# A three-layer recurrence and attention on one core: pipeline offsets of 8 and 16 turns, setup spread over turns, products in even units

## The chip, the cores and the metric

One core of a Trainium2 chip runs the whole program. The metric is the device time in microseconds (us) of one execution; it is given as the median of several runs. TensorE is PE in the profile (PEld is its weight loads), VectorE is DVE, ScalarE is ACT, GpSimd is POOL and SyncE is SP. SP issues most of the DMAs. Line numbers with an L are those of the kernel before.

## The reference, cut to what matters

A batch of 8 sequences of 512 tokens, 512 wide, goes through three recurrent layers and one attention layer. Each adds its output to its input. All numbers are float32.

```
x = x + L0(x)    # gated: needs h of the token before
x = x + L1(x)    # plain tanh recurrence
x = x + L2(x)    # plain tanh recurrence
x = x + L3(x)    # causal attention, 16 heads, one extra "image" key

L0 step: f = sigmoid([x_t, h] @ w_W + w_b); hid, o = split(f)
         m = x_t @ wx_W + wx_b + hid * (h @ wh_W + wh_b)
         h = o * h + (1 - o) * tanh(m)
L1, L2 step: h = tanh(x_t @ Wx + b + h @ Wh)
L3: q, k, v = split(x @ c_attn_w + c_attn_b)
    k_img, v_img = cond @ uk_w.T + uk_b, cond @ uv_w.T + uv_b
    scores = q @ [k_img, k].T / sqrt(32), causal, + mask
    out = softmax(scores) @ [v_img, v] @ c_proj_w + c_proj_b
```

## The kernel before

The program has two parts, one after the other. The first runs the recurrence; the second runs attention.

**Turns.** `turn(s)` (L660) does one token step of every layer that is live in turn s. Layer l works on token s - OFF[l]. With `OFF = (0, 2 * G + 1, 5 * G + 1)` and G = 4 (L22) the later layers are 9 and 21 turns behind layer 0. The loop (L743) runs s from -5 to 532, so after token 511 of layer 0 there are 21 more turns for the later layers. The order of the work on PE, DVE, ACT and POOL is the order in which it is written (a manual schedule); only SP's order is the scheduler's.

In a turn, PE runs in this order: `stream` twice (L547, tiles ph and po: h of layer 0 times its three gate matrices, each float32 product done as bfloat16 parts), `give0` (L490, tile pg0: a quarter of the input product of layer 0 for four coming tokens), `give12` (L503, tile pg1: the same for layers 1 and 2), `stream12` (L563, tile p12: h of the later layers), and `take` (L656, matmuls at L607). Every matmul uses 32 columns of the array; four of them, in the four column groups, run together.

DVE turns ph by 32 x 32 blocks (L572), sums the parts (L578), does the same with po, runs a scan (L688), forms `drop` (L703) and the new h (L704), and splits h into bfloat16 parts (`rest`, L463). ACT computes sigmoid and tanh between these. POOL forms `keep` (L702), which h also needs. When the new h is split, the next turn's ph can start. Then DVE turns and sums p12, ACT computes four tanh (L723), POOL splits the new h of the later layers (`rest` on POOL, L463) and adds it to x (L733): for layer 1 into xb, where layer 2 will read it, for layer 2 into xo.

**Input products.** `chunk_of` (L475) lets a layer's input product start `AHEAD` = G + 1 = 5 turns before the first of its four tokens, one quarter a turn. `given` (L514) turns a finished product into a tile `raw`, and `place` (L522) adds the bias and puts one token's share where the sums at L578 find it, one turn ahead. In a turn POOL does keep, place for layer 0 (two operations, L533), place for the later layers (L537), the x of layer 0 (L712), then the work of the later layers.

**Attention's q, k and v.** When layer 2 has finished a block of tokens (`BLOCKS`: seven of 64, then 32, 16, 16), `finish` (L617) stores x and queues `pieces`: for q and k eight products, for v some with 512 columns, each product made of KC = 4 pieces of four matmuls. `take(count)` runs pieces: one in three of four turns up to s = 511, three a turn after it. A finished product is copied from PSUM by ACT into one of two tiles e (L627, L645) and stored by SP (L631, L647). After the loop a flush (L753) runs what is left, eight pieces at a time.

**Setup.** `setup_loads` (after turn 513) starts the DMAs of attention's weights and masks, in room that layer 0's weights leave. `setup` (after turn 520) computes its constants in one go: the mask in three bfloat16 parts, some index tiles, the image keys (pk, L223), the image values (pi, L235), the output bias (pb, L245), and the mask sums.

**Attention.** `load(0)` (L792) loads q, k and v of batch 0 once the last block is stored. `run(g)` (L1009) works through 32 groups (8 batches of 4 groups with 4 heads each) in three slots: scores (L878, L884), maximum, exponential, transposes, and the products with v. `open_scores` (L841) computes the score of the image key for all four row blocks of a group.

Of the kernel before, what the change touches and what calls it, by code (L numbers as in the profile page):

```python
# [20 lines left out]
G = 4  # L21
OFF = (0, 2 * G + 1, 5 * G + 1)  # L22
AHEAD = G + 1
# [10 lines left out]
def cond_residual_kernel(  # L34
# [81 lines left out]
    def setup_loads():  # L116
# [38 lines left out]
        nc.gpsimd.memset(parts, 0.0)  # L155
# [5 lines left out]
    def setup(psum, tag):  # L161
# [7 lines left out]

        nc.vector.tensor_scalar(m0, m0, LOWEST, None, ALU.max)  # L170
# [10 lines left out]


# [29 lines left out]
        )  # L212

# [6 lines left out]
        for c in range(KC):  # L220
            pk = psum.tile([P, D], F32, tag=tag, name=f"pk_{c}")
# [11 lines left out]
        pi = psum.tile([P, D], F32, tag=tag, name="pi")  # L233
        for k in range(KC):
            nc.tensor.matmul(  # L235
                pi[0:B, :], ct[:, k, :], w_uku[:, 1, k, :], start=(k == 0), stop=(k == KC - 1)
            )
        nc.vector.tensor_tensor(vimg, pi[0:B, :], buv, ALU.add)
        nc.vector.tensor_tensor(vimg, vimg, bv, ALU.subtract)
        nc.vector.tensor_scalar(mt, mt, LOWEST, None, ALU.max)  # L240

        for c in range(KC):
            pb = psum.tile([P, D], F32, tag=tag, name=f"pb_{c}")
# [7 lines left out]
            )  # L251
        masks(0)
        for m in range(NQ - 1):
            beyond(0, m)
# [55 lines left out]
    with ExitStack() as rec:  # L310
# [164 lines left out]
        def chunk_of(l, s):  # L475

            at = s - OFF[l] + AHEAD
            return at - at % G, at % G
# [43 lines left out]
        def place(s, layers):  # L522
# [3 lines left out]
            share = raw[min(layers[0], 1), s - r - AHEAD + KC - 1][..., r * B : (r + 1) * B]  # L526
# [70 lines left out]
        def product(n, name, operands, width, done):  # L597


            ps = []  # L600
            for k in range(KC):
                def piece(k=k):
                    if not ps:
                        ps.append(psq.tile([P, D], F32, tag="q", name=f"pq_{name}"))
                    lhs, rhs = operands(k)
                    for j in range(KC):
                        nc.tensor.matmul(  # L607
                            ps[0][j * BP : (j + 1) * BP, 0:width],
                            lhs[:, j * BP : (j + 1) * BP], rhs,
                            start=(k == 0), stop=(k == KC - 1),  # L610
                        )
                    if k == KC - 1:
                        evict.append(lambda: done(ps[0][:, 0:width]))
                pieces.append(piece)

        def finish(n):
# [6 lines left out]
            for c in range(KC):  # L623
                for i in range(2):
                    def done(p, c=c, i=i):
                        e = ev.tile([P, D], F32, tag="e", name=f"e_{n}_{c}_{i}")
                        nc.scalar.activation(  # L627
                            e[:, 0 : B * size], p, AF.Identity,
                            bias=bcol[:, i, c : c + 1], scale=(qscale, 1.0)[i],
                        )  # L630
# [25 lines left out]
        def take(count):  # L656
            for _ in range(min(count, len(pieces))):
                pieces.pop(0)()

        def turn(s):  # L660
# [17 lines left out]
            take(int(s % 4 > 0) if s < T else 3)  # L678
# [29 lines left out]
            if [l for l in nxt if l]:  # L708
                place(s + 1, [l for l in nxt if l])
# [5 lines left out]
            if later:  # L715
# [12 lines left out]
                rest(nc.gpsimd, new12 if len(later) == 2 else new12[:, later[0] - 1])  # L728
# [6 lines left out]
            given(s, False)  # L735
            n = next((n for n in range(len(BLOCKS)) if s - OFF[2] + 1 == sum(BLOCKS[: n + 1])), None)
# [3 lines left out]
        with tc.manual_schedule(  # L740
            engines={nc.tensor.engine, nc.vector.engine, nc.scalar.engine, nc.gpsimd.engine}
        ):
            for s in range(-AHEAD, T + OFF[2]):  # L743
                n, at = divmod(s + AHEAD + 2 * G, TB)
                if at == 0 and 1 < n < NB:
                    load_x(n)
                turn(s)
                if s == TB:
                    load_qkv()
                if s == T + 1:  # L750
                    setup_loads()
                if s == T + 8:
                    setup(psq, "q")  # L753
            while pieces:
                take(2 * KC)
# [377 lines left out]
```

## Time and profile before

| | us |
|---|---|
| median of 3 runs (3559.51 to 3566.15) | 3562.95 |
| the profiled execution | 3555.52 |
| its span | 3553.4 |
| layer 0's last scan (L688) starts at | 2673.7 |
| last transposition of p12 (L572) starts at | 2796.2 |
| last matmuls of the flush (L607) end at | 2833.5 |
| first scores of attention (L878) start at | 2845.8 |
| PE busy / DVE busy / ACT busy / POOL busy | 3317.1 / 2436.9 / 1417.1 / 1283.2 |

The span lies between the first and the last instruction; the profiled execution's own time is 2.1 us longer. A turn of the recurrence can be read in the timeline from one start of ph to the next. Each line of the timeline has the start, the duration, the engine, the line, the operation with the tiles that it writes and reads, and in brackets the idle time before it and what ended that. In the table by windows, each line has the window, its length, and for every engine the busy time with the number of instructions, then the granted clock of PE, the DMA share and the rate.

### The profile page before, as it was taken

To read this page: it belongs to the slowest core of one execution; us is meant where nothing else is said; L and a number is where in the kernel's file an instruction comes from. 1 tells how busy PE (TensorE), PEld (TensorE's weight loads), DVE (VectorE), ACT (ScalarE), POOL (GpSimd) and SP (SyncE) were. 2 spreads that over 40 slices of the span, in tenths; PEclk is the share of its full clock that TensorE was granted. 3 is DMA by queue.
4 is the path that set the end of the run, shared out by engine and by line. 5 is a ranking of instruction groups with operands and counts; after the bars stand their busy time and mean duration, and the time that the engine had idled before them with its cause. 6 is when DMAs were issued, how large, how long until landed. Compare 5 with 4: busy or idle time off the path is not lost. (4 is left out here: it accounts for less than half of the span.)

```text
span 3553.4 us, 207431 instructions
## 1 busy us (share of the span) xinstructions
PE 3317.1 (93%) x91784; PEld 2417.4 (68%) x91784; DVE 2436.9 (69%) x7061; ACT 1417.1 (40%) x5179; POOL 1283.2 (36%) x4982
## 2 busy tenths in 40 slices
PE   4899999999999999999999999999998679999999
PEld 2677777777777777777777777777774445555555
DVE  4677777777777777777777777777773166777775
ACT  3233333333333333333333333333332156666664
POOL 2444444444444444444444444444442100100000
PEclk9999999999999999999999999999998979999999
DMA  4200010001001000100010001001012221222211
GB/s 126 54 8 7 8 24 18 16 16 34 16 17 28 16 20 17 28 16 19 16 28 16 22 20 25 16 17 28 13 31 50 51 102 53 63 68 73 63 37 25
DMA packets 197771, 116.30 MB, mean 33 GB/s; under 512 B 148684, under 2 KB 165092, under 8 KB 196860
## 3 DMA queue, kind: packets, MB, share of 16 engines
q1 hardware_dynamic: 191880, 100.92, 11.2%
q8 instruction: 721, 11.81, 1.4%
q10 hardware_dynamic: 4992, 2.11, 0.3%
q14 instruction: 178, 1.46, 0.1%
HBM read 61.02 MB, written 41.97 MB: 29 GB/s over the span
## 5 line engine op out<-in xcount | busy, mean ns | idle before, releaser
L547 PEld LDWEIGHTS <-h 128*32 128x32 bf16 x49152 | 1039.9, 97 | 371.8 <-DVE h L463 268.5
L723 ACT ACTIVATE h<-s 64x32 f32<-64x32 f32 x2048 | 535.8, 262 | 974.3 <-DVE s L578 946.7
L547 PE MATMUL ph<-v,h 128*32 128x256 bf16 x24576 | 771.9, 274 | 94.0 <-DVE h L463 79.1
L563 PE MATMUL p<-v,h 128*32 128x256 bf16 x24576 | 786.4, 273 | 20.9 <-POOL h L463 20.4
L463 POOL TENSOR_TENSOR h<-h 128x64 f32<-128x64 f32 (+1 forms) x1048 | 331.0, 316 | 1236.1 <-ACT h L723 1159.6
L563 PEld LDWEIGHTS <-h 128*32 128x32 bf16 x24576 | 674.2, 97 | 149.7 <-POOL h L463 34.3
L572 DVE STREAM_TRANSPOSE s<-ph 128x256 f32<-128x256 f32 x512 | 230.3, 450 | 374.3 <-PE ph L547 374.2
L490 PE MATMUL pg<-w0x,xb 128*32 128x384 f32 x4096 | 427.6, 491 | 24.5 <-DMA w0x<-in_wx_W_dram 10.6
L547 PE MATMUL po<-v0o,h 128*32 128x128 bf16 x24576 | 436.9, 220 | 0.0
L503 PE MATMUL pg<-w12x,xb 128*32 128x256 f32 x4096 | 321.4, 379 | 5.2 <-issue 3.5
L463 DVE TENSOR_TENSOR h<-h 128x32 f32<-128x32 f32 x1036 | 278.5, 270 | 35.9 <-DVE h L704 1.1
L572 DVE STREAM_TRANSPOSE s<-p 128x256 f32<-128x256 f32 (+1 forms) x524 | 232.6, 444 | 81.2 <-PE p L563 81.1
L578 DVE TENSOR_REDUCE sh<-s 128x64 f32<-128x320 f32 x512 | 249.0, 486 | 54.9 <-POOL h L463 2.8
L696 ACT ACTIVATE gates<-sh 128x32 f32<-128x32 f32 x512 | 119.6, 234 | 418.0 <-DVE sh L578 413.5
L607 PE MATMUL pq<-xo,w_qkv 128*32 128x512 f32 (+2 forms) x2560 | 273.4, 515 | 11.5 <-ACT e L627 11.5
L503 PEld LDWEIGHTS pg<-w12x,xb 128*32 128x32 f32 x4096 | 129.7, 110 | 210.6 <-issue 192.6
L578 DVE TENSOR_REDUCE s<-s 128x64 f32<-128x320 f32 (+1 forms) x524 | 254.7, 486 | 19.8
L702 POOL TENSOR_TENSOR keep<-og,h 128x32 f32<-128x32 f32 x512 | 139.8, 273 | 269.1 <-ACT og L699 269.0
L703 DVE SCALAR_TENSOR_TENSOR drop<-og,th 128x32 f32<-128x32 f32 x512 | 112.3, 219 | 155.2 <-ACT th L701 155.2
L878 PE MATMUL s<-qkt 32*128 32x384 f32 (+3 forms) x1024 | 155.3, 491 | 60.6 <-ACT prob L925 35.0
L911 DVE TENSOR_REDUCE rtop<-s 128x2 f32<-128x256 f32 (+3 forms) x256 | 205.0, 821 | 6.7
L975 ACT COPY pt<-tr 128x512 f32<-128x512 f32 x224 | 119.6, 588 | 187.1 <-PE tr L970 186.8
(155 smaller groups left out, 4206.6 us busy)
## 6 DMA issues: line engine op xcount, KB each, us to landing
qkt<-qk_out SPq DMA_DIRECT2D x16, 1024.0 KB, 5.7
qk_out<-e SPq DMA_DIRECT2D x56, 256.0 KB, 3.1
xin<-in_x_dram SPq DMA_DIRECT2D x128, 64.0 KB, 2.0
vt<-v_out SPq DMA_DIRECT2D x8, 1024.0 KB, 5.7
xr<-x_out SPq DMA_DIRECT2D x8, 1024.0 KB
out_dram<-res SPq DMA_DIRECT2D x128, 64.0 KB, 1.7
x_out<-xo SPq DMA_DIRECT2D x28, 256.0 KB, 5.3
v_out<-ev SPq DMA_DIRECT2D x56, 128.0 KB, 2.3
```

The source lines that it names most:

```text
L463: eng.tensor_tensor(part(h, i + 1), part(h, i), top(h, i), ALU.subtract)
L490: nc.tensor.matmul(pg[0][j * BP : (j + 1) * BP, :], tokens(t, c), w[:, j], start=(c == 0), stop=(c == KC - 1),)
L503: nc.tensor.matmul(pg[1][q * BP : (q + 1) * BP, :].rearrange("r (v n) -> r v n", v=2), tokens(t, c), w[:, u], start=(c == 0), stop=(c == K ...
L547: nc.tensor.matmul(out[j * BP : (j + 1) * BP, :], half(h, c), w[:, c, i].rearrange("p (g j n) -> p j g n", g=cols, j=KC)[:, j], start=(c = ...
L563: nc.tensor.matmul(out[q * BP : (q + 1) * BP, :].rearrange("r (v n) -> r v n", v=2), half(h[:, l - 1], c), w[:, u], start=(c == 0 and i == 0),
L572: nc.vector.transpose(to[:, :, :, 0 : NS - 1], p.rearrange("p (k b i) -> p k b i", b=B, i=NS - 1))
L578: nc.vector.tensor_reduce(to, parts, AX.X, ALU.add)
L607: nc.tensor.matmul(ps[0][j * BP : (j + 1) * BP, 0:width], lhs[:, j * BP : (j + 1) * BP], rhs, start=(k == 0), stop=(k == KC - 1),)
L702: nc.gpsimd.tensor_tensor(keep, og, part(old0, 0), ALU.mult)
L723: nc.scalar.activation(part(new12[v * 2 * BP : (v + 1) * 2 * BP, l - 1], 0), s_[fr, v * KC : (v + 1) * KC], AF.Tanh,)
L878: nc.tensor.matmul(pair[g, u, i // 2 * 2][:, i % 2, at : at + n], qkt[b][hs, 0, c, m * P : n], qkt[b][hs, 1, c, 0:n], start=True, stop=False,)
L911: nc.vector.tensor_reduce(top[:, k], s[:, :, at : at + (m + 1) * P], AX.X, ALU.max)
```

## The change

Six things are changed.

1. The offsets are `OFF = (0, 2 * G, 4 * G)`, that is 8 and 16, and the input products of the later layers start 4 turns ahead instead of 5 (`AHEAD = (5, 4, 4)`). The loop ends with turn 527. The input product of the later layers is now turned into `raw` in the same turn in which its first share is placed, so `place` for the later layers moves to the end of POOL's turn, behind `given`.
2. A piece is now a unit of at most 128 columns: a product 512 wide has 16 units instead of 4 pieces. `take` runs 3 units a turn while s < 496, 6 while s < 512, then 12. Units that follow each other in one k are run as one matmul (per column group).
3. `setup_loads` comes after turn 511. `setup` is a generator; from turn 512 on, turn 513 left out, two of its steps follow each turn. Its PSUM tiles are those of po and ph, which layer 0 no longer needs, and the image values are done in two halves.
4. From turn 512 on, the split of the later layers' h is done by DVE instead of POOL.
5. The flush uses matmuls with 128 columns of the array (`whole=True`), up to 16 units at a time; in the last block DVE instead of ACT copies the q products out of PSUM.
6. `load(0)` loads the first 384 tokens from POOL's queue and the last 128 from SP's. The image scores of group 0 are computed for row blocks 0 to 2 first and for block 3 ahead of the third slot. The pools of attention are created in another order, with waits by tile.

```diff
-OFF = (0, 2 * G + 1, 5 * G + 1)
-AHEAD = G + 1
+OFF = (0, 2 * G, 4 * G)
+AHEAD = (G + 1, G, G)
...
         def product(n, name, operands, width, done):
...
+            def stretch(k, at, end, whole=False):
+                if not ps:
+                    ps.append(psq.tile([P, D], F32, tag="q", name=f"pq_{name}"))
+                lhs, rhs = operands(k)
+                if whole:
+                    nc.tensor.matmul(
+                        ps[0][:, at:end], lhs, rhs[:, at:end],
+                        start=(k == 0 and at == 0), stop=(k == KC - 1), skip_group_check=True,
+                    )
+                for j in range(0 if whole else KC):
+                    nc.tensor.matmul(
+                        ps[0][j * BP : (j + 1) * BP, at:end],
+                        lhs[:, j * BP : (j + 1) * BP], rhs[:, at:end],
+                        start=(k == 0 and at == 0), stop=(k == KC - 1), skip_group_check=True,
+                    )
+                if k == KC - 1 and end == width:
+                    evict.append(lambda: done(ps[0][:, 0:width]))
...
-                pieces.append(piece)
+                for at in range(0, width, P):
+                    pieces.append((stretch, k, at))
...
-        def take(count):
-            for _ in range(min(count, len(pieces))):
-                pieces.pop(0)()
+        def take(count, whole=False):
+
+            units = [pieces.pop(0) for _ in range(min(count, len(pieces)))]
+            while units:
+                (stretch, k, at), n = units[0], 1
+                while n < len(units) and units[n] == (stretch, k, at + n * P):
+                    n += 1
+                stretch(k, at, at + n * P, whole)
+                units = units[n:]
...
-            take(int(s % 4 > 0) if s < T else 3)
+            take(3 if s < T - 4 * G else 6 if s < T else 12)
...
             if 0 in nxt:
                 place(s + 1, [0])
-            if [l for l in nxt if l]:
-                place(s + 1, [l for l in nxt if l])
...
-                rest(nc.gpsimd, new12 if len(later) == 2 else new12[:, later[0] - 1])
+                rest(nc.gpsimd if s < T else nc.vector, new12 if len(later) == 2 else new12[:, later[0] - 1])
...
             given(s, True)
             given(s, False)
+            if [l for l in nxt if l]:
+                place(s + 1, [l for l in nxt if l])
...
-                if s == T + 1:
+                if s == T - 1:
                     setup_loads()
-                if s == T + 8:
-                    setup(psq, "q")
+                    bits = setup(pst)
+                if s >= T and s != T + 1:
+                    for _ in range(2):
+                        next(bits, None)
+            for _ in bits:
+                pass
             while pieces:
-                take(2 * KC)
+                take(4 * KC, whole=True)
...
     def load(b):
...
+        cuts = (0, T - P, T) if b == 0 else (0, T)
+        for t0, t1 in zip(cuts, cuts[1:]):
+            eng = nc.sync if t1 == T else nc.gpsimd
+            for i in range(2):
+                eng.dma_start(
+                    qkt[b][:, i, :, t0:t1], qk_out[i, :, :, b, t0:t1].rearrange("c p t -> p c t")
+                )
+            eng.dma_start(
+                vt[b][:, t0 // P : t1 // P], v_out[b, t0:t1].rearrange("(m p) n -> p m n", p=P)
+            )
...
         for u, ks in enumerate(SLOTS):
             before = late[:]
             late.clear()
+            if g < 0 and u == 2:
+                open_scores(0, (3,))
...
         load(0)
-        open_scores(0)
+        open_scores(0, (0, 1, 2))
```

## The prediction

> **What bounds the kernel now.** I read the table by windows first, to see which stages there are.
>
> ```profile
> 1000.00:1500.00 500.00, 491.78 (x16120) 375.07 (x16116) 363.02 (x1118) 177.32 (x704) 225.66 (x875) 1.00 0.09 22
> 2800.00:2850.00 50.00, 25.50 (x448) 16.37 (x448) 2.95 (x10) 5.77 (x15) 0.00 (x0) 0.78 0.52 119
> ```
>
> In the recurrence PE (the first pair) is busy 491.8 of 500 us at full clock; around the flush it is busy half the time at clock 0.78. The timeline of PE shows a turn:
>
> ```profile
> 1501.15 1.03 PE L607 MATMUL pq<-xo,w_qkv 128*32 128x512 f32 x8
> 1502.01 1.48 PE L547 MATMUL ph<-v,h 128*32 128x256 bf16 x48
> 1503.99 0.82 PE L490 MATMUL pg<-w0x,xb 128*32 128x384 f32 x8
> 1505.06 1.48 PE L563 MATMUL p<-v,h 128*32 128x256 bf16 x48
> 1506.92 1.50 PE L547 MATMUL ph<-v,h 128*32 128x256 bf16 x48 [0.38 <-DVE h L463]
> 1508.91 0.82 PE L490 MATMUL pg<-w0x,xb 128*32 128x384 f32 x8
> 1511.30 1.03 PE L607 MATMUL pq<-xo,w_qkv 128*32 128x512 f32 x8
> ```
>
> From start to start: the turn at 1502.01 has no piece and lasts 4.91 us, and PE waits in it for h. Without that wait its work ends at p12 + 1.31 = 4.36. A piece adds 0.86 (1501.15 to 1502.01). Over turns 100 to 479 the timeline gives medians of 5.225 with a piece (285 turns) and 4.907 without (95). So three turns in four are bound by PE (4.367 + 0.858), and the fourth by the chain from ph over DVE and ACT to h. Layer 0's scans 80 and 496 are 2141.06 us apart: 5.147 a turn.
>
> POOL in the same stretch:
>
> ```profile
> 1503.66 0.71 POOL L463 TENSOR_TENSOR h<-h 128x64 f32<-128x64 f32 x2 [2.02 <-ACT h L723]
> 1504.32 0.27 POOL L733 TENSOR_TENSOR xb<-xb,h 128x32 f32<-128x32 f32 x1
> 1505.56 0.28 POOL L702 TENSOR_TENSOR keep<-og,h 128x32 f32<-128x32 f32 x1 [0.73 <-ACT og L699]
> 1506.25 0.31 POOL L537 TENSOR_TENSOR s<-raw,bias 128x64 f32<-128x64 f32 x1
> ```
>
> It is free for 0.73 us before keep. Then the tail, flush and start of attention:
>
> ```profile
> 2684.90 2.68 PE L563 MATMUL p<-v,h 128*32 128x256 bf16 x48 [2.17 <-POOL h L463]
> 2719.94 0.45 DVE L572 STREAM_TRANSPOSE s<-p 128x256 f32<-128x256 f32 x1 [3.50 <-PE p L563]
> 2735.16 5.81 PE L235 MATMUL pi<-room_b,ct 128*8 128x512 f32 x8
> 2749.55 0.45 DVE L572 STREAM_TRANSPOSE s<-p 64x256 f32<-64x256 f32 x1 [0.31 <-PE p L563]
> 2806.28 0.37 ACT L627 ACTIVATE e<-pq,bcol 128x128 f32<-128x128 f32 x1 [5.11 <-DMA qk_out<-e]
> 2820.47 0.37 ACT L627 ACTIVATE e<-pq,bcol 128x128 f32<-128x128 f32 x1 [5.64 <-DMA v_out<-ev]
> 2839.76 1.84 PE L846 MATMUL pim<-kb,qkt 128*128 128x4 f32 x8 [6.23 <-DMA v_out<-ev]
> 2845.83 1.24 PE L878 MATMUL s<-qkt 32*128 32x256 f32 x8 [4.23 <-DMA qkt<-qk_out]
> ```
>
> Two p12 transpositions lie at 2724.66 and 2749.55: 24.89 us for the one turn that holds the setup, against 4.72 for the turn before. The flush waits for stores that free the e tiles, and the first scores wait for the load of q and k.
>
> **Even units.** Three units are 384 of 512 columns: 0.75 x 0.858 = 0.644, and pg0, also 384 wide, measures 0.645 (1508.91 to the next start at 1509.56). A turn of PE is then 4.367 + 0.644 = 5.01. In two turns of four the three units span two k, so a matmul of 128 columns stands alone: 114 such records (14.25 groups of eight) of a product took 3.52 us, 0.247 a group against 0.215, so +0.03, and the mean gains 0.02. The chain must stay below: the new h is split 4.72 to 4.87 after ph starts (median 4.87), plus 0.05 to release PE, so 4.92 at most; it fits with 0.1 to spare.
>
> **The new wait.** With offset 16, layer 2 reads in turn s four tokens of which layer 1 wrote the last in turn s - 1; with 21 it had four more turns. This occurs once in four turns, at the second half of pg12. Layer 1's add into xb ends 7.98 after its turn's ph (median; 7.82 to 8.16). PE would start that half at 5.01 + 2.84 = 7.85. With 0.05 for the semaphore and 0.06 for the weights the wait is 0.1 to 0.4; I take 0.15, because place no longer stands among the operations that overlap the DVE split (the 4.72). p12, the units and the next ph are queued behind it on PE, so it counts in full: 0.04 a turn. Mean turn: 5.01 + 0.02 + 0.04 = 5.07; bounds 5.02 (no wait) and 5.13 (0.4 each time). 416 turns x (5.147 - 5.07) = **-32** (-53 to -7).
>
> The moved place ends POOL's turn: layer 2's add ends at 8.24, place takes 0.31 to 0.40, so 8.55 to 8.64; keep wants POOL at 5.07 + 3.555 = 8.63. It costs nothing as long as the 0.1 of the chain covers it.
>
> Turns 496 to 511 take six units: 4.367 + 1.5 x 0.858 = 5.65, against 75.71 / 15 = 5.05: **+9**. Layer 2 enters five turns earlier, at 0.2 more for each: **+1**.
>
> **Tail.** It runs from layer 0's last scan (2673.7) to the last p12 transposition (2796.2): 122.5 us. After, 16 turns. A turn with both layers and nothing in the way is 4.57 (2715.37 to 2719.94). But ACT copies products out before it does the tanh, and so waits until the units are through: 2701.70 to 2708.42 is 6.72 with a copy that waited for the third piece. The same sum with 12 units (2.58) and DVE's split (two operations of 0.3 instead of 0.69 on POOL) gives 5.5 where a product ends at 1.72 and 6.4 where it ends at 2.58. Turns 512 to 515: 5.5, 6.4, 5.5, 6.4. Turn 516 follows nine DVE operations of the mask and index steps (2.7 + 1.9 us by their rows): 7.0. Turn 517 has two pk, of which the second waits for DVE: 6.2. 518 and 519: 5.6, 6.5. Together 49. Layer 2 alone: 3.9 unhindered (2753.37 to 2757.26). Turn 520 has three copies of 0.37, the third waiting for an e tile (2.4 us to landing), and two pb: 7.4; 521: 6.3; 522 and 523: 5.3, 5.2; four at 3.8. Together 39. The setup's PE work (pk, pi, pb: 16 us, mostly at half clock) lies in the time in which PE waits for the tanh, except in turns 517 and 520, counted above; without that cover it would cost up to 16. setup_loads comes two turns earlier: SP issues 29 DMAs, the 16 of w_proj at 0.65 to 2 us, ahead of one or two stores of e. They are covered by the 14 us from one copy to the next; if not, one ACT copy and the tanh behind it lose up to 7.
>
> The clock: p12 took 2.68 instead of 1.49 after 2.17 us of idle PE (first line of the last fence); after 1.8 it ran at 1.16 for one layer, full speed. Turns 524 to 527 have no units, so PE idles 2.7 us in each, and I add 0.9 x 4 = 3.5. [...]
>
> 1.6 (rest of turn 511) + 49 + 39 + 3.5 = 93 to 95: **-28**. Bounds: 16 free turns (8 x 4.57 + 8 x 3.9 = 68) give -53; all 16 at 6.7 give -14.
>
> **Flush.** 2796.2 to 2833.5 is 37.3 us with 17 copies out of PSUM, 2.19 each, most of it the wait for an e tile's store. After, only the last block's 48 units are left, which are eight copies of q and k and one of v: 9 x 2.19 = 20: **-17**. Matmuls on the whole array change little: 117.6 us for 128 matmuls of 512 columns at L825 is 0.92, against 0.86 for four in parallel. Bounds: 9 copies at 3.5 (each waits its store in full) is -6; 1.2 each is -26.
>
> **Start of attention.** The first scores come 12.3 us after the flush's last matmul. The first 384 tokens can be loaded as soon as the last p12 has read the weights that lie in that room, some 20 us before the flush ends. No load on POOL's queue is in the trace; SP's of 1024 KB land after 5.7 us, and three of 768 KB should not need more than 17. Behind them on POOL stands nothing until `shares` of group 0. Then the first scores wait only for the last copy out of PSUM: 0.6, plus six image matmuls at half clock, 1.4: 2.5 after the flush. The last part lands some 9 us after it (v's eight stores issue until +6, +3 to land), and the third slot comes at +12. **-10** (0, if it is not covered, to -11).
>
> **Sum.** -32 + 9 + 1 - 28 - 17 - 10 = -77. Profiled execution: 3555.5 - 77 = 3478. It lies 7.4 below the median of the runs, and below all three, so I carry that over: 3563 - 77 = **3486**. The rest of attention is left as it is.
>
> **Rivals.** (A) The forecast, 3486, by itself 3465 to 3510: chance 0.68. (B) The evening gives nothing: layer 2's wait is 0.4 or more and the late keep lengthens the chain, so turns stay at 5.15: 3486 + 32 = 3518. For it: POOL's slack is below 0.1 by the rows; against it: a late keep first uses up the chain's own 0.1. 0.12. (C) Better: layer 2's wait is hidden (5.02, 21 less) and the tail runs near its free turns (20 less): 3445. For it: the 4.72 and 7.82 at the low end; against: the 6.72 turn. 0.13. (D) The early load is not early (it waits for the last stores, or POOL is slow to issue it): 3496. 0.04. (E) **Slower.** POOL becomes the loop: place now stands between layer 2's add and keep. From keep's start to the next ph are 1.36 us, so a turn of 5.28 needs keep at 3.92, 0.36 late in every turn, which means a place that ends at 9.2 instead of 8.6. From there on 416 x 0.13 eats the other 45 us and the whole is slower; with another 0.02 it is 3572. For it: a POOL split of 1.01 instead of 0.69 (2727.62, beside DVE's setup work); against: that is the only one, and it is half of what is needed. 0.03.
>
> **Range and chances.** About 0.2% (7 us) can be told from no change. (B) and half of (C) are to be held: 3446 to 3528. Faster: (A) to (D), less a little: 0.94; same 0.02; slower 0.04, with (E).
>
> **What would show it.** Right: turns of 5.05 to 5.1 of one length, with PE waiting once in four turns 0.1 to 0.2 us at the second half of pg12 for POOL; 16 tail turns in 94 us with no 25 us turn; nine copies in the flush; first scores 2 to 3 us after its last matmul. Wrong: turns of 5.15 or more with keep late; pk or pi waiting for a weight DMA; a copy waiting longer than 5 us in the tail; first scores still waiting for qkt.

## The result: a third of the gain that was forecast

The changed kernel takes 3535.29 us (median of four runs, 3534.39 to 3542.97) against 3562.97 for the kernel before on the same chip: a ratio of 0.9929, 95% interval 0.9917 to 0.9941, 27.7 us. The forecast was 77. In a later set of runs (`after_again`, below) it was 0.9959, 0.9943 to 0.9975.

One profiled execution of each kernel can mislead here: the changed kernel's first one was the slowest of its four. So the stages stand below for two executions of each; the times are read from the same marks as in the prediction (layer 0's scans 80, 496 and 511, the last p12 transposition, the flush's last matmul, the first scores, the end).

| stage, us | before | before, again | after | after, again | forecast of the change |
|---|---|---|---|---|---|
| up to scan 80 | 456.9 | 454.9 | 458.4 | 458.5 | +1 |
| scans 80 to 496 | 2141.1 | 2142.2 | 2135.6 | 2143.2 | -32 |
| scans 496 to 511 | 75.7 | 76.0 | 84.0 | 83.9 | +9 |
| to the last p12 transposition | 122.5 | 120.9 | 111.5 | 112.2 | -28 |
| flush | 37.3 | 35.2 | 25.1 | 25.4 | -17 |
| to the first scores | 12.3 | 12.2 | 1.4 | 1.4 | -10 |
| attention from there | 707.6 | 721.3 | 725.2 | 714.1 | 0 |

Three rows are nearly as forecast (496 to 511, the first scores, the start). The attention differs by 13.7 us between two executions of the same kernel, so its 17.6 us of the first pair show nothing. What is missing lies in the steady turns (about 30 us), the tail (some 18) and the flush (some 6).

The table by windows of the kernel after (each window's length, then busy time and instructions of PE, PE's weight loads, DVE, ACT, POOL, then PE's clock and DMA):

```profile
1000.00:1500.00 500.00, 499.84 (x16818) 440.05 (x16811) 362.10 (x1124) 184.81 (x708) 236.23 (x879) 1.00 0.09 22
2780.00:2830.00 50.00, 27.39 (x185) 20.80 (x181) 11.90 (x34) 7.02 (x27) 3.91 (x8) 0.74 0.52 134
```

PE is busy without a gap, 499.84 of 500 us, and yet the turns are hardly shorter. The figures in brackets are what the prediction did not read: 16818 matmuls where before had 16120, in almost the same number of turns (500 / 5.134 = 97.4 against 500 / 5.147 = 97.1). That is 172.7 a turn against 166.0.

Turns with the new wait, in the timelines of PE and of POOL of the kernel after:

```profile
1601.30 1.49 PE L560 MATMUL ph<-v,h 128*32 128x256 bf16 x48
...
1606.31 1.49 PE L560 MATMUL ph<-v,h 128*32 128x256 bf16 x48
1608.93 0.76 PE L516 MATMUL pg<-w12x,xb 128*32 128x256 f32 x6
1609.53 0.39 PE L516 MATMUL pg<-w12x,xb 128*32 128x256 f32 x2
```

```profile
1608.31 0.71 POOL L476 TENSOR_TENSOR h<-h 128x64 f32<-128x64 f32 x2 [2.37 <-ACT h L754]
1608.97 0.27 POOL L764 TENSOR_TENSOR xb<-xb,h 128x32 f32<-128x32 f32 x1
```

The last two records of pg12 begin 3.22 us after ph instead of 2.84, once layer 1's add of the turn before (POOL, L764, ended 1609.24) is there. The wait is where it was forecast, and larger: 0.36 us in each fourth turn by the medians of scan to scan (5.37 against 5.01 to 5.02 in the other three), not 0.15. The add itself is not late: it ends 4.9 us after the scan of its turn by the median, as in the kernel before, and in the turns shown 7.94 us after its ph (1601.30), where 7.98 was forecast. What differs is the time at which PE would have gone on. Each f32 matmul stands in the trace as two records (the four of pg12 as eight), and in the kernel before all eight records of pg12 lie in one group:

```profile
1504.63 0.60 PE L503 MATMUL pg<-w12x,xb 128*32 128x256 f32 x8
```

The first records of both halves start there at 1504.63 to 1504.64, 2.62 us after the ph at 1502.01; 2.84 is where the second records start. From 5.01 + 2.62 = 7.63 to the forecast end of the add and 0.05 for the semaphore (in the turn shown, from the add's end at 1609.24 to the first record of the held half at 1609.29) are 0.4 us, the upper end of the span that the prediction gave.

Tail, flush and first maxima, in the timelines of ACT, DVE, SP and POOL of the kernel after:

```profile
2699.06 0.47 ACT L649 ACTIVATE e<-pq,bcol 128x256 f32<-128x256 f32 x1 [5.59 <-DMA qk_out<-e]
2751.16 0.37 ACT L649 ACTIVATE e<-pq,bcol 128x128 f32<-128x128 f32 x1 [3.23 <-DMA qk_out<-e]
```

```profile
2804.28 0.35 DVE L654 TENSOR_SCALAR e<-pq,bcol 128x128 f32<-128x128 f32 x1 [10.24 <-DMA qk_out<-e]
2821.51 1.02 DVE L958 TENSOR_REDUCE rtop<-s 128x2 f32<-128x256 f32 x2 [3.46 <-DMA v_out<-ev]
```

```profile
2689.82 0.43 SPq L139 DMA_DIRECT2D room_b<-in_uv_wT_dram  x1
2690.35 9.72 SPq L658 DMA_DIRECT2D qk_out<-e  x3
...
2791.55 5.61 SPq L643 DMA_DIRECT2D x_out<-xo  x4
2797.26 15.11 SPq L658 DMA_DIRECT2D qk_out<-e  x8
```

```profile
2791.85 1.74 POOL L837 DMA_DIRECT2D qkt<-qk_out  x2 [0.32 <-issue]
2793.58 0.75 POOL L840 DMA_DIRECT2D vt<-v_out  x1
```

Before the tanh of turn 513 ACT waits 5.59 us for a store that SP issued only after the setup's loads, at 2690.35, and whose packets (128 bytes each) move from 2695.7 on, while those of the loads move from 2688.6 to 2696.5. From its transposition of p12 to the next one, that turn takes 11.98 us. In the flush the third copy waits 10.24 us. The early load runs there: it was issued at 2791.85, x_out's stores at 2791.55, and SP came to the first store of e at 2797.26.

### The profile page after: what moved, and what is told of

It is laid out like the page before. It is cut to its first block, busy times and chain, and to the rows that moved or that the text cites. A ratio compares the mean times of both kernels' runs of the same rounds, so it can differ in the third digit from the quotient of the medians.

```text
span 3541.2 us, 211969 instructions
## 1 busy us (share of the span) xinstructions
PE 3356.8 (95%) x94136; PEld 2713.3 (77%) x94136; DVE 2425.4 (68%) x7092; ACT 1436.4 (41%) x5175; POOL 1319.3 (37%) x4944
## 3 DMA queue, kind: packets, MB, share of 16 engines
q0 software_dynamic: 592, 2.36, 0.2%
q14 instruction: 179, 1.46, 0.1%
## 5 line engine op out<-in xcount | busy, mean ns | idle before, releaser
L560 PEld LDWEIGHTS <-h 128*32 128x32 bf16 x49152 | 1117.3, 97 | 168.1 <-DVE h L476 97.1
L576 PE MATMUL p<-v,h 128*32 128x256 bf16 x24576 | 884.3, 274 | 21.5 <-DVE h L476 19.9
L560 PE MATMUL ph<-v,h 128*32 128x256 bf16 x24576 | 851.8, 274 | 45.4 <-DVE h L476 29.9
L576 PEld LDWEIGHTS <-h 128*32 128x32 bf16 x24576 | 762.0, 97 | 92.6 <-ACT h L754 24.4
L560 PE MATMUL po<-v0o,h 128*32 128x128 bf16 x24576 | 518.7, 220 | 7.3 <-issue 7.2
L503 PE MATMUL pg<-w0x,xb 128*32 128x384 f32 x4096 | 489.1, 493 | 23.5 <-DMA w0x<-in_w_W_dram 13.6
L516 PE MATMUL pg<-w12x,xb 128*32 128x256 f32 x4096 | 425.2, 381 | 5.6 <-DVE raw L533 3.8
L516 PEld LDWEIGHTS pg<-w12x,xb 128*32 128x32 f32 x4096 | 214.5, 110 | 167.9 <-issue 73.5
L625 PE MATMUL pq<-xo,w_qkv 128*32 128x128 f32 (+3 forms) x4056 | 335.3, 376 | 0.5 <-issue 0.5
L476 DVE TENSOR_TENSOR h<-h 128x32 f32<-128x32 f32 (+1 forms) x1068 | 240.4, 226 | 76.7 <-ACT h L754 40.5
L958 DVE TENSOR_REDUCE rtop<-s 128x2 f32<-128x256 f32 (+3 forms) x256 | 205.0, 821 | 10.1 <-DMA v_out<-ev 3.5
## 6 DMA issues: line engine op xcount, KB each, us to landing
xr<-x_out SPq DMA_DIRECT2D x8, 1024.0 KB, 10.2
```

Source lines behind the costliest of these rows:

```text
L476: eng.tensor_tensor(part(h, i + 1), part(h, i), top(h, i), ALU.subtract)
L503: nc.tensor.matmul(pg[0][j * BP : (j + 1) * BP, :], tokens(t, c), w[:, j], start=(c == 0), stop=(c == KC - 1),)
L516: nc.tensor.matmul(pg[1][q * BP : (q + 1) * BP, :].rearrange("r (v n) -> r v n", v=2), tokens(t, c), w[:, u], start=(c == 0), stop=(c == K ...
L560: nc.tensor.matmul(out[j * BP : (j + 1) * BP, :], half(h, c), w[:, c, i].rearrange("p (g j n) -> p j g n", g=cols, j=KC)[:, j], start=(c = ...
L576: nc.tensor.matmul(out[q * BP : (q + 1) * BP, :].rearrange("r (v n) -> r v n", v=2), half(h[:, l - 1], c), w[:, u], start=(c == 0 and i == 0),
L625: nc.tensor.matmul(ps[0][j * BP : (j + 1) * BP, at:end], lhs[:, j * BP : (j + 1) * BP], rhs[:, at:end], start=(k == 0 and at == 0), stop=( ...
```

## The experiments

Each kernel is the changed one with the edit shown. The ratio is to the kernel before, on the same chip in the same set; sets are named where they are compared.

**1. The wait for layer 1's add.** Three kernels and the changed one again, one set.

> The changed kernel once more, unchanged. The profiled execution of the first time was the slowest of its four (3542.97 against a median of 3535.29), and its attention took 725.2 us against 707.6 before. Theory 1 (attention lost time by the change: the first groups start with PE at half clock and wait for a store of v): the first three groups again take 50.8, 25 and 24 us, some 10 more than before, and the other groups 20 to 21.5; time 3534 to 3537. Rival (the 17.6 us are that one execution): attention within 3 us of 707.6.

```
-    rest(nc.gpsimd if s < T else nc.vector, ...)
-    for l in later: ...
+    if later[0] == 1:
+        add(1)
+    rest(nc.gpsimd if s < T else nc.vector, ...)
+    if later[-1] == 2:
+        add(2)
```

> POOL adds layer 1's h into xb ahead of the split of layers 1 and 2 instead of behind it, which takes 0.69 us out of the way of layer 2's tokens. Theory 1 (the one long turn in four, 5.38 us, is PE's wait at the second half of pg12 for that add): all four turns at 5.01 to 5.05, the mean from 5.134 to 5.02 to 5.05, layer 0's scans 80 to 496 in 2090 to 2100 us instead of 2135.6, time 3490 to 3505. Rival (the long turn comes from DVE or ACT, which transpose pg and copy products out in that turn, or from a split that ends 0.27 later and so holds p12): the long turn stays above 5.25 and the time within 3530 to 3545.

```
-OFF = (0, 2 * G, 4 * G)
+OFF = (0, 2 * G, 5 * G)
```

> Layer 2 runs 20 turns behind layer 0 instead of 16, so that its tokens are four turns old when PE reads them. Theory 1 (the wait for layer 1's add is what evening the units lost): turns at 5.01 to 5.05 and scans 80 to 496 in 2086 to 2100 us, 36 to 50 less than the changed kernel; four turns more with layers 2 and products after the last scan, 4 to 8 us each: time 3505 to 3520. Rival (evening itself is worth next to nothing): scans 80 to 496 in 2125 us or more, time 3545 to 3560.

```
-            take(3 if s < T - 4 * G else 6 if s < T else 12)
+            take(4 * int(s % 4 > 0) if s < T - 4 * G else 6 if s < T else 12)
```

> The changed kernel with the units of a product taken as before up to turn 495: a whole piece of four in three turns of four, none in the fourth. Theory 1 (the wait for layer 1's add takes the evening's gain; with whole pieces the turn that waits is the one without a piece, whose end is set by the chain to h at 4.92 anyway, so the wait costs little): turns of 5.14 to 5.20 on average, scans 80 to 496 in 2138 to 2163 us, time 3537 to 3563, so evening with the wait is worth 2 to 28 us. Rival (with the new offsets the wait is not the limit, uneven units cost nothing): scans 80 to 496 below 2130 us, time below 3532.

| | time, us | ratio (95%) | scans 80 to 496 | mean turn | mean of the four medians |
|---|---|---|---|---|---|
| after_again | 3547.46 | 0.9959 (0.9943 to 0.9975) | 2143.2 | 5.152 | 5.096 |
| add_first | 3523.71 | 0.9903 (0.9878 to 0.9929) | 2137.6 | 5.139 | 5.029 |
| off20 | 3535.28 | 0.9926 (0.9914 to 0.9938) | 2128.8 | 5.117 | 5.027 |
| whole_pieces | 3529.24 | 0.9910 (0.9897 to 0.9922) | 2134.2 | 5.130 | 5.112 |

Theory 1 fails, and so does its rival. With the wait taken away, by order or by offset, all four kinds of turn have the medians of the forecast (5.01 to 5.07), but the mean stays at 5.12 to 5.14: 45 us (add_first) and 38 us (off20) lie in single turns, some hundred of the 416 in each, that are 0.2 to 1.4 us longer. And with whole pieces, as before the change, scans 80 to 496 take no longer than with even units (2134.2 against 2135.6 and 2143.2), and the kernel is 18 us faster than after_again: the evening gains nothing. (add_first's profiled execution is 15.9 us shorter than after_again's, of which only 5.6 lie in scans 80 to 496; 5.7 come before them and 5.3 in the tail.) after_again meets neither of its two expectations: its attention takes 714.1 us, its first three groups take 50.8, 21.7 and 20.8, and its time lies above the 3534 to 3537 expected. The kernel before took 721.3 for its attention in its second execution (run `before_again` below).

What the long turns are shows in PE's timeline of off20, in the middle of one group:

```profile
1126.41 0.77 PE L560 MATMUL po<-v0o,h 128*32 128x128 bf16 x39
1127.86 0.34 PE L560 MATMUL po<-v0o,h 128*32 128x128 bf16 x9 [0.68 <-issue]
```

PE stands 0.68 us between two matmuls of one product, which wait for nothing that the profile names. The view of waits, over 460 to 2590 us, has none of these for the kernel before (its only row is 36.2 us of ph for h), and in add_first, longest rows (line and what it waited for: us in total, times, longest):

```profile
PE po L560 <- issue: 9.7, 27, 0.7
PE p L576 <- issue: 3.1, 11, 0.4
```

All rows of this kind in add_first add up to 15.7 of its 45 us; the groups around a pause run longer too (in the turn of off20 above p12 takes 1.72 us and ph 1.58, where 1.49 is usual).

The DMA records name what is late. One queue, listed in the trace as `instruction`, moves packets of 16384 bytes, and its count follows PE's: over 460 to 2590 us PE has 561 times 256 instructions in off20, and the queue 562 packets; in the kernel before it is 539 and 539. In all 31 pauses of more than 0.25 us in add_first, and in all 25 of off20, PE goes on 1.2 to 1.6 us after the last such packet has landed, while the packets come some 3.8 us apart.

**2. PE's supply of instructions.** Theory 3: with no gap left, the stream of instructions is the bound. A kernel with fewer instructions, and a bare measurement.

```
-            take(3 if s < T - 4 * G else 6 if s < T else 12)
+            take(3 if s < T - 4 * G else 6 if s < T else 12, whole=True)
```

> POOL's add ahead of the split (as in add_first), and up to turn 511 each stretch of a product is one matmul on the whole array instead of four on a quarter: some 12 of PE's 336 instructions a turn less. In add_first the four kinds of turn have medians of 5.01 to 5.07, as forecast, but the mean is 5.139: 45 us lie in turns that are 0.25 to 1 us longer, in which PE stands between matmuls of one group and goes on 1.3 to 1.5 us after a 16 KB packet of the instruction queue has landed. Theory 3 (with PE busy all the time, its stream of instructions is what runs dry): with 3.6% fewer instructions and units some 0.04 dearer the medians are 5.03 to 5.08, the excess over them falls from 45 to under 20 us, scans 80 to 496 in 2095 to 2120 us, time 3495 to 3512. Rival (the excess comes from stores that fill the DMA engines, or from the clock): excess stays above 35 us, scans 80 to 496 in 2140 us or more, time 3525 to 3545.

```
+            probe = psq.tile([P, D], F32, tag="q", name="probe")
+            for i in range(4096):
+                j = i % KC
+                nc.tensor.matmul(
+                    probe[j * BP : (j + 1) * BP, 0:P], three[:, j * BP : (j + 1) * BP], three,
+                    start=(i < KC), stop=(i >= 4096 - KC),
+                )
```

> The changed kernel with 4096 small bf16 matmuls (32 x 128 out, each with a weight load) put behind the flush, so 8192 instructions for PE without a wait; their result is not used. Theory 3 (PE's instructions come in 16 KB packets, 256 of them, at a pace of their own): the stretch takes 32 x 3.2 to 3.4 = 102 to 109 us, the packets follow each other at the smallest distance seen so far (3.23 us), and PE stands every 256 instructions. Rival (the stream keeps up with any pace): 4096 matmuls at 14 ns, as in the groups of po (48 in 0.67 us), take 57 to 60 us.

The probe, in PE's timeline:

```profile
2869.79 1.97 PE L798 MATMUL probe<-three 128*32 128x128 bf16 x128 [1.78 <-issue]
2873.54 1.97 PE L798 MATMUL probe<-three 128*32 128x128 bf16 x128 [1.78 <-issue]
2877.01 1.97 PE L798 MATMUL probe<-three 128*32 128x128 bf16 x128 [1.50 <-issue]
```

128 matmuls and their 128 weight loads run in 1.97 us; then PE stands for 1.5 to 1.8 us, and the next 128 come 3.75 us after the last (3.47 to 4.02, from 2856 us on). The whole stretch took 123 us, longer than the 102 to 109 expected, because the pace is 3.75 and not 3.3, and because at its start, while the last stores of v and the first batch's load ran, the next 128 came 4.6 to 6.5 us after the last. So in the probe PE gets 256 instructions every 3.75 us, 68 in a microsecond; the run `unmerged` (below) holds 3.73 over its whole loop. Between 2856 and 2940 us 22 such stretches begin, and the queue `instruction` moves 22 packets.

add_whole is slower, 3616.68 us (ratio 1.0162, 1.0143 to 1.0180): its turns are all 5.33, since three units on the whole array take 0.85 where four quarters side by side took 0.64 to 0.65 (add_first), and p12 ends 0.1 later ahead of them. That price was put at 0.04 and is 0.3, so the expected times are missed. On what it was to tell apart it is clear. PE works without a pause in it too, but for one of 0.4 us between 460 and 2590:

```profile
1507.04 1.49 PE L560 MATMUL ph<-v,h 128*32 128x256 bf16 x48
...
1510.11 1.48 PE L576 MATMUL p<-v,h 128*32 128x256 bf16 x48
1511.52 0.92 PE L620 MATMUL pq<-xo,w_qkv 128*128 128x256 f32 x4
1512.37 0.84 PE L560 MATMUL ph<-v,h 128*32 128x256 bf16 x24
```

and the excess over the medians is 0.5 us in 416 turns, under like data traffic (21 GB/s between 1000 and 1500 us, 22 in add_first) and at a like granted clock (0.980 over the execution, 0.983 in add_first, which has 45 us). A turn of 327 instructions at 5.33 us leaves 4.17 us for each 256.

**3. The count of instructions alone.** Even turns without the odd cuts, and whole pieces cut up.

```
-            take(3 if s < T - 4 * G else 6 if s < T else 12)
+            take((2, 2, 4, 4)[s % 4] if s < T - 4 * G else 6 if s < T else 12)
```

> The changed kernel with 2, 2, 4, 4 units in the four kinds of turn up to turn 495, so that no group of 512 columns is cut at an odd place: four matmuls a turn instead of four or eight, 337 instructions of PE a turn instead of 345. Theory 4 (PE is fed 256 instructions every 3.80 us at best in this loop, 3.75 in the probe; the changed kernel's 345 a turn take 5.12 by that, its PE work only 5.01): 337 x 3.80 / 256 = 5.00, so PE's work sets the turn again, two turns at 5.22 and two at 4.80 to 4.85, mean 5.01 to 5.05, scans 80 to 496 in 2084 to 2101 us, time 3490 to 3508. Rival (the turn is held by the chain to h or by layer 1's add, not by instructions): mean 5.10 or more, time 3525 to 3545.

```
+            take(4 * int(s % 4 > 0) if s < T - 4 * G else 6 if s < T else 12, merged=s >= T)
...
-                while n < len(units) and units[n] == (stretch, k, at + n * P):
+                while merged and n < len(units) and units[n] == (stretch, k, at + n * P):
```

> Whole pieces (as in whole_pieces) whose four units are each matmuls of their own up to turn 511: 369 instructions of PE a turn on average instead of 333, the same products. Theory 4: 369 x 3.80 / 256 = 5.48 us a turn, scans 80 to 496 in 2255 to 2300 us. Rival (only PE's work counts: units of 128 columns take 0.247 instead of 0.215, so 0.13 more in three turns of four): 5.20 to 5.25 a turn, 2165 to 2185 us.

> The kernel before, once more, for its attention: 707.6 us in the first profiled execution, against 714 to 726 in eight executions of kernels with the change. Theory (the change costs the attention some 7 us, at the first groups): 706 to 710 again. Rival (the attention differs from one execution to another by PE's granted clock): 713 or more.

halves takes 3515.02 us, ratio 0.9859 (0.9846 to 0.9873), with a mean turn of 5.071 and scans 80 to 496 in 2109.3. The turns have the medians forecast (4.85, 4.80, 5.22, 5.23), the mean is 0.045 above them; the expected stretch is missed by 8 us and the time by 7, but both are far from the rival's. Its wait for layer 1's add is nearly hidden (4.85 against 4.80 us), so the kernels to compare it with are add_first and off20, which have no such wait and medians of the same mean (5.03): they need 2137.6 and 2128.8 us. These differences are larger than those between executions: the loop of halves, which best3 to best5 (below) have too, takes 2109.3 to 2114.3 us in four executions, and that of the changed kernel 2135.6 to 2143.2 in five (after, after_again, probe, ring4, one_load).

unmerged takes 5.384 us a turn and 2239.7 for scans 80 to 496, below the expected 2255. That is 0.1 below what theory 4 gave with 3.80 us for each 256 instructions, and 0.13 above the highest value of the rival, for which only PE's work counts; with the probe's 3.75 theory 4 gives 5.41. Its three turns with a piece have the same work for PE, and yet their medians rise from 5.42 over 5.51 to 5.59, behind a turn without a piece of 4.78. A dearer matmul would lengthen all three alike. In all its 78 pauses of more than 0.25 us PE again goes on 1.2 to 1.6 us after a packet has landed.

before_again: 3564.82 us, attention 721.3, so the rival holds: one execution's attention differs from another's by more than the change does.

The runs side by side (instructions of PE a turn: matmuls, weight loads and a few semaphore instructions between 460 and 2590 us, over the turns there; an f32 matmul counts as two matmuls and two weight loads; the last two columns go over scans 80 to 496, in us):

| | instructions a turn | at 3.75 us for 256 | mean of the four medians | measured mean |
|---|---|---|---|---|
| add_whole | 327 | 4.80 | 5.328 | 5.330 |
| before | 333 | 4.88 | 5.148 | 5.147 |
| whole_pieces | 333 | 4.88 | 5.112 | 5.130 |
| halves | 337 | 4.94 | 5.026 | 5.071 |
| after | 345 | 5.06 | 5.106 | 5.134 |
| add_first | 345 | 5.06 | 5.029 | 5.139 |
| off20 | 345 | 5.05 | 5.027 | 5.117 |
| unmerged | 369 | 5.41 | 5.327 | 5.384 |

Where the third column is 0.2 or more below the fourth, the measured mean stays within 0.02 of the medians' (add_whole, before, whole_pieces); halves, 0.09 below, lies 0.045 above them; where the third column comes within 0.05 of the fourth or passes it, the mean leaves the medians by 0.03 to 0.11 and lies between 0.03 below and 0.08 above the third column. In the kernel after the wait for layer 1's add falls into time that the instructions take anyway: with it 5.134 to 5.152 in five executions, without it 5.139.

**4. Tail and flush.**

```
+        def e_tile(name):
+            taken.append(name)
+            k = len(taken) % 4
+            if k > 1 and "room_b" in made:
+                at = HG * 10 * P + (k - 2) * D
+                return made["room_b"][:, at : at + D]
+            return ev.tile([P, D], F32, tag="e", name=name)
```

> The changed kernel with four e tiles from turn 511 on instead of two (two of them in room that the weights of layer 0 have left). Theory (the copies out of PSUM wait for stores that SP issues late, behind the loads of the setup and behind the stores of x_out: 5.59 us in turn 513, 3.23 in turn 520, 10.24 in the flush): these waits are gone, the 16 turns behind the last scan take 100 to 105 us instead of 111.5, the flush 13 to 18 instead of 25.2, the time falls by 12 to 22 us. Rival (the waits only come last beside others: PE at half clock, DVE's mask steps): tail above 108, flush above 22, time within 5 us of the changed kernel.

```
-        cuts = (0, T - P, T) if b == 0 else (0, T)
+        cuts = (0, T)
```

> The changed kernel with the first batch loaded in one part by SP behind the flush, as before. Theory (the early load on POOL's queue collides with the last stores, and what it gives the first scores is lost again in the flush and in the first three groups): flush 18 to 22 us instead of 25.2, first scores 10 to 13 us behind it instead of 1.4, first group 45 to 48 instead of 50.8, time 0 to 5 us above the changed kernel. Rival (no collision; the store waits for SP, which issues x_out): flush stays at 24 to 26, first scores at +10 to +13, time 8 to 12 us above the changed kernel.

ring4: 3531.51 us, ratio 0.9917 (0.9894 to 0.9940). The tail takes 101.5 us, as expected (turn 513 6.4 instead of 12, turn 520 7.3 instead of 12.5), the flush 23.4, as the rival has it: one copy still waits 8.15 us. By the ratios it is 4 to 15 us below the changed kernel, against 12 to 22 expected. one_load, which also computes the image scores of group 0 in one go again, takes 3541.16 us, 0.9951 (0.9936 to 0.9966). Its flush takes 18.0 us and the first scores come 10.1 later. So the early load gives the start 8.7 us and takes 7.2 from the flush. Its first group takes 49.0 us, counted to the end of its last matmul; since this is 47.4 to 54.1 in the other executions, no gain or loss there is shown.

**5. A better version, and what holds the flush.** best3 is halves with ring4's edit, small pools of the attention that wait tile by tile (`reuse_waits="tile"` for ptp and a3), and x_out's last stores emitted behind the flush.

> halves, four e tiles from turn 511 on (as in ring4), the last block's stores of x_out behind the flush instead of ahead of its stores of q, k and v, and the attention's small pools waiting tile by tile. Theory: the gain of halves, some 10 us in the tail (101 instead of 111.5), a flush of 14 to 18 us (SP took 5.61 us to issue x_out and 5.45 for the next two stores), and 3.5 us at the first maxima, which waited for a store of v: time 3462 to 3485. Rival (the flush and the first maxima wait for POOL's early load and for PE's clock): only the gain of halves and of ring4, 3480 to 3500.

3495.78 us, 0.9805 (0.9792 to 0.9818), 11 us above the range of its theory. The tail falls to 95.8 and the first maxima no longer wait (0.04 us, against 3.6 in halves), but the flush stays at 23.6: SP, whose order is not written by hand, issued three of the four x_out stores first all the same. Two kernels on that:

```
-                store_x()
+                store_x(nc.gpsimd)
```

> best3 with the last block's four stores of x_out issued by POOL, ahead of the early load, since SP issued three of them first all the same. Theory A (SP, held by x_out's stores, issues the stores of e late): e stores are issued from the start of the flush on, the flush takes 13 to 17 us instead of 23.6, the early load still lands before its first use, time 6 to 11 us below best3 (3495.8). Theory B (the early load of 2.36 MB and the stores share the DMA engines, and the load fills them for 7 us): the flush stays above 20 us, time within 4 us of best3.

> best3 without the early load: the first batch is loaded in one part by SP behind the flush, and x_out's stores stand where they stood. Theory A (SP and x_out's stores hold the flush): it stays above 20 us and the first scores come 9 to 12 us later, time 8 to 12 us above best3. Theory B (the early load holds it): flush 14 to 18 us, first scores 9 to 12 us behind it, time within 5 us of best3, so that the two-part load is worth nothing where it stands.

best4: 3496.22 us, 0.9812 (0.9799 to 0.9825), flush 25.1. best5: 3493.75 us, 0.9805 (0.9792 to 0.9819), flush 14.6, first scores 10.2 behind it. Theory B holds in both. SP's queue and one copy on DVE in best4:

```profile
2754.07 2.04 SPq L674 DMA_DIRECT2D qk_out<-e  x2
2757.29 2.19 SPq L674 DMA_DIRECT2D qk_out<-room_b  x2
2759.58 8.81 SPq L674 DMA_DIRECT2D qk_out<-e  x2
```

```profile
2769.03 0.35 DVE L670 TENSOR_SCALAR room_b<-pq,bcol 128x128 f32<-128x128 f32 x1 [9.79 <-DMA qk_out<-room_b]
```

and SP's in best5:

```profile
2758.35 1.69 SPq L668 DMA_DIRECT2D qk_out<-room_b  x2
2760.41 1.46 SPq L668 DMA_DIRECT2D qk_out<-e  x2
```

In best4 SP has nothing ahead of its stores and issues them from 2754 on; when the load's data flows (337 GB/s on average between 2760 and 2767), two stores take 8.81 us to be issued and a copy waits 9.79. Without the load two stores take 1.46. best3 and best5 are both some 69 us below the kernel before and, by their ratios, 44 to 55 below the changed one.

## Why the prediction was wrong, point by point

**Even units: the step that failed.** "A turn of PE is then 4.367 + 0.644 = 5.01 [...] so a matmul of 128 columns stands alone [...] +0.03, and the mean gains 0.02." As PE's time this is right: the medians of add_first and off20 are 5.01 to 5.07. As a turn it is wrong, because the odd cuts add on average six f32 matmul records and six weight loads a turn, 333 to 345 instructions, and PE is fed some 256 in 3.75 us (the probe's pace): 5.06 for the turn, more than its work of 5.03, and 5.12 to 5.15 measured. The prediction counted what the cut costs on the array and not what it costs in instructions, though the counts stood in the first line of the profile that it showed. It also took the turns of the kernel before as if PE's work alone set them with nothing close behind; the supply was, at 4.88. At the same work for PE, eight instructions a turn fewer (halves against add_first and off20) take 20 to 28 us out of scans 80 to 496, most of the some 30 us missing, and bring them to 2109.3, where the forecast had them. The sum by the supply is not closed, though: 5.06 alone would have left the forecast of 5.07 standing. In after, after_again, add_first and off20, where supply and work lie 0.03 apart, the mean is 0.06 to 0.09 above the larger of the two. Packets that come late would explain it (in the kernel after they land 3.2 to 5.9 us apart, 3.76 by the median); that is argued, not shown.

Rival B ("the evening gives nothing") is what happened there, but not by its mechanism. Its wait of 0.4 or more nearly came true (0.36), but without that wait (add_first) the turns are no shorter. Its late keep did not come: keep starts 3.55 us after ph, as forecast, and PE waits for h in no turn of the stretch.

**The new wait** was mis-sized (0.15 forecast, 0.36 measured): "PE would start that half at 5.01 + 2.84 = 7.85" takes the second records of the half for its first, which start at 2.62. The 0.06 that it adds for the weights is the author's estimate and shows in no run: in the turn shown the first record of the held half begins 0.05 after the add's end, and its weights with it. For now it costs nothing that can be seen, since it lies in time that the instruction stream needs (2137.6 us without it, in add_first, 2135.6 to 2143.2 with it).

**Turns 496 to 511** (+9) came out at +8.3 and +7.9, **layer 2 earlier** (+1) at +1.5 to +3.6.

**Tail.** Forecast -28, measured -11 and -9. The step that failed is "They are covered by the 14 us from one copy to the next; if not, one ACT copy and the tanh behind it lose up to 7." They are not covered. With 12 units a turn and 8 in a product, two products end in turn 513, and the second one's copy, which needs the tile of turn 512's copy, could start 4.7 us after that one's end (2688.78 to 2693.46), not 14. SP reaches the store of e only behind the setup's loads, and the copy waits 5.59 us. The wait in turn 520 is another: its store is issued at once, at 2747.09, and the copy waits 3.23 us for it, where the prediction had 2.4 to landing. Behind both waits p12 takes 2.75 and 2.77 us instead of 1.49. With four e tiles the tail takes 95.7 to 101.5 us; forecast were 94.5. The 7.0 for turn 516 behind the mask steps is 9.0 (from the transposition of p12 in turn 515 to that in 516). On the clock, PE's p12 after 2.28 us of idle ran 2.75 us in turn 525, at a granted clock of 0.51, and 1.49 after 2.36 in turn 526, at 1.00. So an idle time of 2.3 us stood ahead of half the clock in one turn and of the full clock in the next, and the row that the prediction went by (2.68 us after 2.17 of idle) does not tell which.

**Flush and start.** -17 and -10 were priced each on its own. Each holds alone: without the early load the flush is 18.0 us (20 forecast), with it the first scores come 1.4 us behind the flush (2.5 forecast). Together their packets are moved at the same time (between 2791 and 2801 us of the kernel after those of the load's queue take 66.5% of the time of the 16 DMA engines, those of SP's queue 15.7%; in best4, between 2760 and 2767, 87.4% and 14.1%), and the flush is 25.1. The prediction looked at what stands behind the load on POOL's queue and not at whose transfers run beside it. best4 and best5 show what that does: two stores take 8.81 us to be issued beside the load, 1.46 without it.

**Attention.** 0 forecast; 725.2 and 714.1 after, 707.6 and 721.3 before, which shows no change. The first maxima do wait 3.46 us for a store of v, whose tile's room they take; that is gone in best3, and in one_load too (0.03).

What stays open: in the loop of the changed kernel the supply runs at 3.80 to 3.82 us for 256 instructions, in that of unmerged at 3.73; halves stays 0.045 above its medians. That PE runs through its instructions in the short turns of 4.80 us faster than they come would explain the second: 14.6 of the 18.6 us lie in the two short kinds of turn, which have 337 instructions as well and would need 4.94 at the probe's pace. It was not tried.

## What to carry to other kernels

When an engine is busy without a gap, count its instructions: here 345 a turn met a supply of 256 in 3.75 us, and the odd cuts took back what the even turns gave. Before splitting matmuls to fill holes, divide the instructions of a turn by that pace and compare it with the turn aimed at. And price two transfers that are moved beside each other together, not one by one.

## What was not expected of the hardware

- PE's instructions come in 16 KB packets through the DMA engines (539 packets for 539 times 256 instructions in the loop of the kernel before). With 4096 small matmuls in a row, PE worked 1.97 us and stood 1.78 in each 3.75; with heavy data traffic beside it (269 GB/s between 2831 and 2851), 4.6 to 6.5 us passed from one packet's worth to the next.
- Products of 384 f32 columns cost 0.85 us on the whole array (add_whole) and 0.64 to 0.65 as four quarters side by side (add_first), so fewer instructions were not free here.
- A DMA's issue can take long on the issuing engine: two stores of 64 KB took 8.81 us on SP while a 2.36 MB load ran from POOL's queue (best4), 1.46 without it (best5).
